# A conditional layer in quarters of the array, 512 columns at a time, turned by DMA

## The chip, the cores and the metric

The kernel runs on one core of one Trainium2 chip. The metric is the device time of one execution in microseconds: the median of 3 runs before the change is 2462.17 us (2460.88 to 2463.17). A separate, profiled execution gives the trace. Engines are named as in the profile: PE (TensorE) multiplies matrices, PEld is its weight load, DVE is VectorE, ACT is ScalarE, POOL is GpSimd, and SP issues most of the DMAs.

## What is computed

64 samples of 64 rows and 1024 columns pass one layer. Sample `b` is first multiplied by one of 16 small matrices, chosen by a list; then attention with 32 heads over 64 positions, an output projection with a residual, a second conditional layer and a quantised feed-forward follow. The change touches only the first step.

```python
W = weights[condition]                       # (64, 64, 64): one 64x64 matrix per sample
y = jnp.einsum('bct,bcd->bdt', x, W)         # the conditional layer
qkv = y @ attn_qkvw + attn_qkvb              # 1024 -> 3 x 1024
q, k, v = split_into_32_heads_of_32(qkv)
probs = softmax((q @ k.T) / sqrt(32))        # per sample and head, 64 x 64
x = x + (probs @ v) @ attn_ow + attn_ob
x = x + ffn(cond2(x))
```

All of this is in float32 up to the feed-forward.

## The kernel before

**Tiling.** The 4096 rows (tokens) go in 8 blocks of 512, and a block in four tiles of 128 rows, two samples each. A block's conditional output `y` is kept transposed, columns of `y` on the partitions, as four quarters `B11`, `B12`, `B21`, `B22` (first number: half of the 1024 columns; second: half of the block's 512 tokens). The projections to q, k and v use a Winograd-like scheme with seven products instead of eight; it needs four sums of the quarters, `T1` to `T4`. `T4` takes the place of `B12`.

**The conditional layer** (`conditional`, L339 on). For each tile j and half hf four matmuls (L355) hold 128 columns of x as weights and pass `wbd[j]`, a 128x128 matrix with the two samples' 64x64 matrices on its diagonal. The result arrives transposed, in one PSUM tile of 512 columns. DVE (L361) or ACT (L363) copies it into `yB`, and DVE makes the sums (L371, L376). POOL fills `wbd` in later blocks (L380), DVE in the first.

**Order of work.** Everything is issued from one program written out by hand. A planned clock `now` advances by a cost for each product on PE; `at(time, f)` puts work due at a planned time, and `run` issues what is due before the next product. An engine runs its own instructions strictly in this order. The order is thus fixed, and the times are only a plan: scores and contexts, for example, have no cost in it. Each block has four phases c = 0 to 3. A phase holds two groups of scores (L498), at its start and its middle, each for two of four units, and fills PE between them with projection jobs: q and k jobs of seven products of 1.72 us, v jobs of seven products of 3.43 us. Phase 0 has q, v and k; phases 1 and 2 have q and k; phase 3 has the next block's conditional layer, its first v job and its first q and k jobs.

A group goes: scores on PE; maximum, subtraction on DVE; exponent on ACT (L514); sum, reciprocal and product on DVE; `ph`, a split into 16-bit halves, on ACT (L528); `phT`, a DMA transpose issued by SP (L533); `pT`, the join of the halves, on ACT (L540), planned 8 us after the transpose; later the contexts on PE (L550) and `co` on ACT (L561). Contexts are taken two at a time, when two groups are ready, so some groups have none.

**Buffers that tie engines together.** Products go through four PSUM buffers (`ps_g`). In a q or k job ACT copies the first product (`psqp`, `pskp`, L406) and later takes the fifth, which lies in the same buffer, with its bias (`qT`, or four pieces of `kbd`, L419); the next job's first product needs that buffer again. The scores of a phase's first group read, in their second half, the `kbd` that ACT wrote. Contexts have two PSUM buffers (`ps_c`).

**Queues.** SP issues in program order the weights (`wq`, `wk`, 1.8 MB each, as soon as the job before the last is done; `wv`, 0.5 MB, after each v product), the x tiles (L246, four at a block's start) and the DMA transposes. POOL issues the gathers of the small matrices (L248) and runs side work ("chores") on the second layer's weights. The pool `xp` has four buffers.

Of the kernel before, what the change touches and what calls it, by code (L numbers as in the profile page):

```python
# [11 lines left out]
F32 = mybir.dt.float32  # L12
BF16 = mybir.dt.bfloat16
I32 = mybir.dt.int32
I16 = mybir.dt.int16
AF = mybir.ActivationFunctionType
ALU = mybir.AluOpType
# [3 lines left out]
P = 128  # L21
# [70 lines left out]
def planes(x):  # L92

    return x.bitcast(I16).rearrange("p (n h) -> p h n", h=2)
# [88 lines left out]
def attention(tc, a, x_t, ctx_d, ident, dram, ps_g, KC, PB, NBLK, NCH, HPC, H, C, chores, early, op):  # L183
# [6 lines left out]
    nc = tc.nc  # L190
    BLK = PB * P
    HB = BLK // 2
    KQ = KC // 2
    NP = NCH // 2
# [4 lines left out]
    cw = a["condw"].rearrange("s c d -> (s c) d")  # L199
# [11 lines left out]
    with ExitStack() as ctx, ExitStack() as mid:  # L211
        def pool(stack, name, bufs, **kw):
            return stack.enter_context(tc.tile_pool(name=name, bufs=bufs, reuse_waits="tile", **kw))
# [9 lines left out]
        yp = pool(mid, "y1", 1, side="right")  # L223
        p1 = pool(mid, "p1", 1, side="right")
        w = pool(early, "w1", 1)
        xp = pool(early, "xp", 4)


        cond_i = w.tile([P, KC * 4], I32, tag="cond_i", name="cond_i")
# [6 lines left out]
        nc.vector.tensor_copy(row_f, row_i)  # L236
        nc.vector.tensor_scalar(idx, cond_i, float(C), row_f, ALU.mult, ALU.add)

        def load_x(b):
            tiles = []  # L240
            for j in range(PB):
                i = b * PB + j
                xt = xp.tile([P, H], F32, tag="x", name=f"x_{i}")
                if i == PB - 1:
                    held(xt[:, 0:1], tiles[0][0])
                nc.sync.dma_start(xt, x_t[i])  # L246
                wg = xp.tile([P, C], F32, tag="wg", name=f"wg_{i}")
                nc.gpsimd.indirect_dma_start(  # L248
                    out=wg[:, :],
                    out_offset=None,  # L250
                    in_=cw,
                    in_offset=bass.IndirectOffsetOnAxis(ap=idx[:, i:i + 1], axis=0),
                )
                tiles.append((xt, wg))
            return tiles

        def held(word, other):


            nc.scalar.copy(word, other[:, 0:1])  # L260
# [24 lines left out]
        def load_qk(b, wh, c, eng=None):  # L285
            t = w_qk[b, wh, c] = wp.tile([P, 7, KQ, P], F32, tag="wqk", name=f"w{wh}_{b}_{c}")
            if b == 0:
                if (wh, c) == ("q", 0):
                    held(t[:, SLOT["A11"], 0, 0:1], x_next[0][1])
                for key in RAW:  # L290
                    nc.sync.dma_start(t[:, SLOT[key], :, :], quarter(key, (0 if wh == "q" else H) + c * P, P))
                return sums(
                    eng or nc.vector, lambda key: t[:, SLOT[key], :, :], lambda: nc.gpsimd.dma_start(qk_d[wh, c], t)
                )
            nc.sync.dma_start(t, qk_d[wh, c])
# [18 lines left out]
            return sums(eng, at, stored)  # L314

        bqkv = act.tile([P, 3 * KC], F32, tag="bqkv", name="bqkv")
        x_next = load_x(0)
        first_sums = load_qk(0, "q", 0) + load_qk(0, "k", 0, nc.gpsimd)
        nc.sync.dma_start(bqkv, a["qkvb_t"])
        first_sums += load_v_raw(0, nc.gpsimd)  # L320
# [1 line left out]

        wbd = []
        for j in range(PB):
            t = w.tile([P, P], F32, tag=f"wbd{j}", name=f"wbd{j}")
            nc.vector.memset(t, 0.0)
            wbd.append(t)
        kbd, vbd = [], []  # L330
        for u in range(4):
            t = act.tile([P, 2, HB], F32, tag=f"kbd{u}", name=f"kbd{u}")
# [6 lines left out]

        B = {}  # L340

        def conditional(b, tiles):

            def one(hf, j):
                key = f"B{hf + 1}{j // 2 + 1}"
                box = []

                def product():
                    xt = tiles[j][0]
                    if j % 2 == 0:  # L350
                        B[key] = yp.tile([P, KQ, HB], F32, tag=key, name=f"y{key}_{b}")
                    ps = ps_g.tile([P, 4, P], F32, tag="g", name=f"cond_{b}_{j}_{hf}")
                    for q in range(KQ):
                        k = hf * KQ + q
                        nc.tensor.matmul(ps[:, q, :], xt[:, k * P:(k + 1) * P], wbd[j], start=True, stop=True)  # L355
                    box.append(ps)

                def rest():
                    dst = B[key][:, :, (j % 2) * P:(j % 2 + 1) * P]
                    if j % 2 == 0:  # L360
                        nc.vector.tensor_copy(dst, box[0])  # L361
                    else:
                        nc.scalar.copy(dst, box[0])  # L363
                    if (hf, j) == (0, 3):
                        t_of("T1", "B12", "B11")
                    elif (hf, j) == (1, 3):
                        t_of("T2", "B22", "T1")
                        t_of("T3", "B22", "B12")
                    elif (hf, j) == (1, 1):
                        B["T4"] = B["B12"]  # L370
                        nc.vector.tensor_tensor(B["T4"], B["B21"], B["T2"], ALU.subtract)  # L371
                return 0.95, product, rest

            def t_of(key, x, y):
                B[key] = yp.tile([P, KQ, HB], F32, tag=key, name=f"{key}_{b}")
                nc.vector.tensor_tensor(B[key], B[x], B[y], ALU.subtract)  # L376

            for j, (_, wg) in enumerate(tiles):
                for r in range(2):
                    (nc.gpsimd if b else nc.vector).tensor_copy(wbd[j][halves[r], halves[r]], wg[halves[r], :])  # L380
            return [one(0, j) for j in range(PB)] + [one(1, j) for j in (2, 3, 0, 1)]

        def job(name, cost, n, matmuls, put, begin=None, done=None, order=ORDER):

# [186 lines left out]
        now = 0.0  # L571
# [3 lines left out]
        def at(time, f):  # L575
            heapq.heappush(due, (time, next(seq), f))
# [2 lines left out]

        def contexts(least=1):  # L580
            ready = sum(len(pTs) == 2 for *_, pTs in waiting)
            for n in range(ready if ready >= least else 0):
                context(*waiting.pop(0), 1.7 * n * (least - 1))

        def group(b, c, us):


            def begin():
                ps = scores(b, c, us)
                if behind:  # L590
                    behind.pop()()
                contexts(2)
                pTs = []
                waiting.append((b, c, us, pTs))
                for n, u in enumerate(us):
                    at(now + 1.7 * n, lambda n=n, u=u: first(u, ps[n], pTs))
                if b > 0:
                    at(now + 8.7, lambda: next(chores, None))
                    if c in (0, NP - 1):
                        at(now + 15, lambda: next(chores, None))  # L600

            def first(u, ps, pTs):
                p = exponents(b, c, u, ps)
                at(now + 3.4, lambda: normalize(b, c, u, p))
                at(now + 6.8, lambda: second(u, p, pTs))

            def second(u, p, pTs):
                h = parted(b, c, u, p)
                at(now + 1.7, lambda: third(u, turned(b, c, u, h), pTs))

            def third(u, hT, pTs):
                at(now + 8, lambda: pTs.append(joined(b, c, u, hT)))
            return begin
# [41 lines left out]
        def with_sums(fills, i, sums, count):  # L655
            cost, product, rest = fills[i]

            def product_and_sums():
                for _ in range(min(count, len(sums))):
                    sums.pop(0)()  # L660
                product()
            fills[i] = (cost, product_and_sums, rest)
# [14 lines left out]
                with_sums(js, 4, pending_sums, 4)  # L677
            return js

        for f in conditional(0, x_next):  # L680
            run(*f)
        for f in first_sums:
            f()
# [2 lines left out]
        for f in qk_fill(0, 0) + v_fill(0, 0):  # L686
            run(*f)
        for b in range(NBLK):
            if b + 1 < NBLK:
                x_next = load_x(b + 1)  # L690
            for c in range(NP):
                fills, length = [], None
                if c + 1 < NP:
                    fills += qk_fill(b, c + 1)
                    if c == 0:
                        fills[7:7] = v_fill(b, 1)
                        if b == 0:
                            for at_ in range(3, 7):
                                with_sums(fills, at_, v_raw, 1)
                elif b + 1 < NBLK:  # L700

                    fills += conditional(b + 1, x_next) + v_fill(b + 1, 0) + qk_fill(b + 1, 0)
                else:
                    behind.pop()()
                    mid.close()
                    op.open_rest()
                    fills += op.pair(0) + op.pair(1)
                    length = 24
                    at(now + 20, contexts)
                if b + 1 == NBLK and c == 1:  # L710
                    assert next(chores, None) is None
                    early.close()
                    for n, load in enumerate(op.open_weights()):
                        at(now + 5 * n, load)
                phase(b, c, fills, length or sum(f[0] for f in fills))
# [971 lines left out]
```

## Time and profile before

| | |
|---|---|
| median of 3 runs | 2462.17 us |
| profiled execution, whole / span | 2461.01 / 2459.1 us |
| mean granted clock of PE | 0.995 |
| attention blocks (68 to 1386 us): PE, DVE, ACT busy | 1315.9, 831.4, 547.3 of 1318 us |
| DMA share in the same stretch | 0.69 |
| PE, conditional layer L355 | 512 records, 61.7 us |
| ACT `ph` L528, `pT` L540 | 1047 ns, 1342 ns each |
| DVE `yB` L361, ACT `yB` L363 | 684 ns, 588 ns each |
| x tile, issue to landing | 9.1 us median, 512 KB |
| `wq`, `wk`, issue to landing | 7.7, 8.1 us median, 1792 KB |

A float32 matmul shows as two records on PE. "Idle before" names what an engine waited for just before an instruction. The times in the tables are those of the one profiled execution.

### The profile page before, as it was taken

The numbers are of one execution on the slowest core, as the hardware profiler recorded it, in microseconds if no ns is written. First come the engines' busy times: TensorE is split into PE (matmuls) and PEld (weight loads), VectorE is DVE, ScalarE is ACT, GpSimd is POOL, SyncE is SP. The second block draws the span as 40 slices with busy tenths as digits, with TensorE's granted clock in tenths as the row PEclk, the third lists the DMA queues.
The fourth block names the chain that finished last, engine by engine and source line by source line (L and its number), as shares of the span: only waits on it lengthen the run. The fifth ranks groups of instructions, "written<-read, shape, count | busy, mean of one in ns | idle before, by whom it ended". The sixth has DMA issues, their size and how long they took to land.

```text
span 2459.1 us, 34200 instructions
## 1 busy us (share of the span) xinstructions
PE 2423.2 (99%) x13194; PEld 1699.6 (69%) x13232; DVE 1533.1 (62%) x2957; ACT 952.8 (39%) x1303; POOL 363.4 (15%) x451
## 2 busy tenths in 40 slices
PE   8999999999999999999999999999999999999996
PEld 7888888888888888888888544444454545454452
DVE  4685585775664755745646623333367777778787
ACT  1353353342443533534424544344323333333333
POOL 5110001011122221210000233333200000000001
PEclk9999999999999999999999999999999999999998
DMA  8895767676677767775547588876744344434343
GB/s 280 284 264 152 219 200 238 188 208 210 201 198 250 206 194 246 207 208 175 177 137 234 170 258 255 263 243 215 242 126 83 84 79 88 80 81 87 70 95 72
DMA packets 417980, 446.76 MB, mean 182 GB/s; under 512 B 299665, under 2 KB 353938, under 8 KB 404114
## 3 DMA queue, kind: packets, MB, share of 16 engines
q1 hardware_dynamic: 387298, 377.90, 52.9%
q0 software_dynamic: 12080, 49.82, 7.7%
q10 hardware_dynamic: 18432, 16.79, 2.0%
q8 instruction: 106, 1.74, 0.3%
q14 instruction: 64, 0.52, 0.1%
HBM read 272.97 MB, written 100.66 MB: 152 GB/s over the span
## 4 chain that ended last, share of the span: by engine, by line
PE 94%; DVE 2%; ACT 2%; DMA 1%; issue 0%; ACTq 0%; SPq 0%; DVEq 0%
PE psva L462 5%; PE pska L435 5%; PE psvd L462 5%; PE psqa L435 5%; PE psvc L462 4%; PE pbc L1031 4%; PE pba L1031 4%; PE psqc L435 4%; PE pskc L435 4%; PE psqd L435 4%; PE pskd L435 4%; PE pbd L1031 4%; PE poa L1031 4%; PE pod L1031 4%; PE poc L1031 4%; PE s L498 3%
## 5 line engine op out<-in xcount | busy, mean ns | idle before, releaser
L540 ACT COPY pT<-phT 128x1024 int16<-128x1024 int16 x128 | 167.2, 1342 | 84.8 <-DMA phT<-ph 84.6
L514 ACT ACTIVATE prob<-prob 128x512 f32<-128x512 f32 x128 | 80.6, 630 | 259.4 <-DVE prob L511 232.1
L421 DVE SCALAR_TENSOR_TENSOR kbd<-pskd,bqkv,psku 32x256 f32<-32x256 f32 x256 | 123.1, 481 | 31.6 <-PE pskd L435 27.8
L528 ACT COPY ph<-prob 128x1024 int16<-128x1024 int16 x128 | 130.8, 1047 | 24.3 <-DVE prob L522 23.7
L1152 POOL TENSOR_TENSOR xo<-xo,ob 128x1024 f32<-128x1024 f32 x32 | 84.1, 2648 | 351.7 <-DVE To L1042 305.5
L561 ACT ACTIVATE co<-c,bqkv 128x256 f32<-128x256 f32 x128 | 60.1, 469 | 179.6 <-PE c L550 152.1
L435 PE MATMUL psqa<-yB,wq 128*128 128x256 f32 x512 | 123.6, 384 | 0.5 <-ACT psqp L406 0.5
L435 PE MATMUL pska<-yB,wk 128*128 128x256 f32 x512 | 122.6, 382 | 0.0
L1495 POOL DMA_DIRECT2D out_dram<-y x29 | 25.2, 869 | 652.3 <-DVE y L1487 652.3
L1126 ACT COPY xh<-xo 128x1024 int16<-128x1024 int16 x64 | 64.1, 1040 | 142.4 <-DVE xo L1171 142.4
L462 PE MATMUL psva<-wv,yB 128*128 128x256 f32 x512 | 117.0, 382 | 0.4
L1031 PE MATMUL poa<-woA,cx 128*128 128x512 f32 x256 | 115.4, 593 | 0.0
L1031 PE MATMUL pba<-wtA,x1T 128*128 128x512 f32 x256 | 115.1, 592 | 0.0
L1137 ACT COPY xTo<-xhT 128x1024 int16<-128x1024 int16 x64 | 84.7, 1339 | 58.4 <-DMA xhT<-xh 52.1
L435 PEld LDWEIGHTS pska<-yB,wk 128*128 128x128 f32 x512 | 96.0, 190 | 15.0 <-issue 2.6
L435 PEld LDWEIGHTS psqa<-yB,wq 128*128 128x128 f32 x512 | 95.2, 190 | 16.0 <-issue 2.8
L462 PEld LDWEIGHTS psva<-wv,yB 128*128 128x128 f32 x512 | 96.1, 190 | 14.1 <-ACT yB L363 1.0
L510 DVE TENSOR_REDUCE mx<-s 128x8 f32<-128x512 f32 x128 | 87.7, 685 | 10.7 <-PE s L498 9.3
L511 DVE TENSOR_TENSOR prob<-s,mx 128x512 f32<-128x512 f32 x128 | 88.5, 691 | 9.3 <-DVE mx L510 0.5
L522 DVE TENSOR_TENSOR prob<-prob,den 128x512 f32<-128x512 f32 x128 | 88.5, 692 | 4.4
L520 DVE TENSOR_REDUCE den<-prob 128x8 f32<-128x512 f32 x128 | 86.7, 678 | 7.2 <-ACT prob L514 6.3
L1031 PEld LDWEIGHTS poa<-woA,cx 128*128 128x128 f32 x256 | 48.4, 190 | 60.1 <-issue 59.9
(243 smaller groups left out, 5135.5 us busy)
## 6 DMA issues: line engine op xcount, KB each, us to landing
wv<-v_d SPq DMA_DIRECT2D x98, 512.0 KB, 3.9
wq<-q_d SPq DMA_DIRECT2D x28, 1792.0 KB, 7.7
wk<-k_d SPq DMA_DIRECT2D x28, 1792.0 KB, 8.1
x<-in_x_dram SPq DMA_DIRECT2D x32, 512.0 KB, 9.1
ctx_d<-co ACTq DMA_DIRECT2D x128, 128.0 KB, 4.2
cx<-ctx_d SPq DMA_DIRECT2D x16, 1024.0 KB, 6.9
xo<-in_x_dram SPq DMA_DIRECT2D x32, 512.0 KB, 5.7
xT_d<-xTo SPq DMA_DIRECT2D x64, 256.0 KB, 3.2
```

Source lines behind the costliest of these rows:

```text
L421: nc.vector.scalar_tensor_tensor(dst, ps, bias, u, ALU.add, ALU.add)
L435: nc.tensor.matmul(ps[:, 0:HB], A[:, SLOT[A_OF[i]], k, :], B[B_OF[i]][:, k, :], start=first and k == 0, stop=k == KQ - 1, skip_group_check ...
L462: nc.tensor.matmul(ps[:, j * VC:(j + 1) * VC], B[B_OF[i]][:, k, j * P:(j + 1) * P], A[:, k, :], start=first and j == 0 and k == 0, stop=k ...
L510: nc.vector.tensor_reduce(mx_v, ps, AX.X, ALU.max)
L511: nc.vector.tensor_tensor(p.rearrange("p (a e) k -> p a e k", a=2), ps, mx_v.unsqueeze(3).to_broadcast([P, 2, HPC, C]), ALU.subtract)
L520: nc.vector.tensor_reduce(den, p, AX.X, ALU.add)
L522: nc.vector.tensor_tensor(p, p, den.unsqueeze(2).to_broadcast([P, n, C]), ALU.mult)
L528: nc.scalar.copy(h, planes(p.rearrange("p n k -> p (n k)")))
L540: nc.scalar.copy(planes(pT.rearrange("p a b q -> p (a b q)")), hT)
L1031: self.nc.tensor.matmul(ps, self.B[self.B_OF[i]][:, k, :], self.A[self.A_OF[i]][:, k, :], start=first and k == 0, stop=k == self.KQ - 1, s ...
L1137: nc.scalar.copy(planes(xT.rearrange("p k q -> p (k q)")), hT)
L1152: nc.gpsimd.tensor_add(s["x"][:, t, :], s["x"][:, t, :], self.ob)
```

## The change

The first block's conditional layer stays as it is. For later blocks it becomes one call per tile, `conditional_tile`, and the tiles are spread over the block before. The small matrices are now the weights: four matmuls with 64x64 weights, one in each quarter of the array, pass 512 columns of x each. Their result is not transposed; so ACT splits it into 16-bit halves (`yh`, one buffer), SP issues a DMA transpose (`yhT`), and ACT joins the halves into the quarter of `y`. For the second half of the columns the two samples lie crosswise, and the join takes two copies. The plan puts the transpose 1.7 us after the split, and the join 5.1 us after the transpose.

A tile is issued in a group that takes no contexts, right after its scores, and once in each block's phase 0 as a fill of its own. It uses the two `ps_c` buffers, and after its matmuls it loads the x tile two ahead. Quarters now have two sets of buffers, one for even and one for odd blocks; `xp` has two x buffers. The sums T1 to T4 move to the end of phase 2 and the first two products of phase 3. Phase 3 has no conditional layer any more. At the start x tiles 2 and 3 and `wbd` borrow buffers of quarters, and the four memsets of `wbd` become one of 128x1024.

```diff
-        xp = pool(early, "xp", 4)
+        xp = pool(early, "xp", 2)
...
-        wbd = []
-        for j in range(PB):
-            t = w.tile([P, P], F32, tag=f"wbd{j}", name=f"wbd{j}")
-            nc.vector.memset(t, 0.0)
-            wbd.append(t)
+        wbd = yp.tile([P, KC, P], F32, tag="B21", name="wbd")
+        nc.vector.memset(wbd, 0.0)
...
+        def conditional_tile(b, j):
+            xt, wg = x_of.pop((b, j))
+            ps = [ps_c.tile([P, 2, HB], F32, tag="c", name=f"cond{hf}_{b}_{j}") for hf in range(2)]
+            for hf in range(2):
+                for r in range(2):
+                    nc.tensor.matmul(
+                        ps[hf][halves[r ^ hf], :, :], wg[halves[r], :], xt[halves[r], hf * 512:(hf + 1) * 512],
+                        start=True, stop=True,
+                    )
+            if j + 2 < PB:
+                load_x(b, j + 2)
+            elif b + 1 < NBLK:
+                load_x(b + 1, j + 2 - PB)
+
+            def parted_y(hf):
+                h = w.tile([P, 2, 512], I16, tag="yh", name=f"yh_{b}_{j}_{hf}")
+                nc.scalar.copy(h, planes(ps[hf].rearrange("p a t -> p (a t)")))
+                at(now + 1.7, lambda: turned_y(hf, h))
+
+            def turned_y(hf, h):
+                hT = w.tile([P, 2, 512], I16, tag="yhT", name=f"yhT_{b}_{j}_{hf}", bufs=2)
+                nc.sync.dma_start(
+                    hT.rearrange("p h (k q) -> p (h k) q", q=P), h.rearrange("p h t -> p (h t)"), transpose=True
+                )
+                at(now + 5.1, lambda: joined_y(hf, hT))
+
+            def joined_y(hf, hT):
+                key = f"B{hf + 1}{j // 2 + 1}"
+                if j % 2 == 0:
+                    Y[key] = quarter_of(b, key)
+                src = hT.rearrange("p h (k q) -> p h k q", q=P)
+                for r in range(2) if hf else (slice(0, P),):
+                    q = halves[r ^ hf] if hf else r
+                    q = slice((j % 2) * P + q.start, (j % 2) * P + q.stop)
+                    dst = Y[key].bitcast(I16).rearrange("p k (q h) -> p h k q", h=2)[:, :, :, q]
+                    nc.scalar.copy(dst, src[:, :, :, halves[r] if hf else r])
+
+            at(now + 1.7, lambda: parted_y(0))
+            at(now + 5.1, lambda: parted_y(1))
...
-                contexts(2)
+                if not contexts(2) and (b, c, us[0]) != (0, 0, 0):
+                    next_tile()
...
+            if b == 0:
+                load_x(1, 0)
+                load_x(1, 1)
             if b + 1 < NBLK:
-                x_next = load_x(b + 1)
+                tiles_to_come += [(b + 1, j) for j in range(PB)]
...
+                        n = 7 if b else 14
+                        fills[n:n] = [(0.9, next_tile, None)]
+                    if c + 2 == NP and b + 1 < NBLK:
+                        sums_to_come = [lambda b=b, n=n, Y=Y: t_of(b + 1, Y, *T_OF[n]) for n in range(4)]
+                        with_sums(fills, -2, sums_to_come, 1)
+                        with_sums(fills, -1, sums_to_come, 1)
                 elif b + 1 < NBLK:
-                    fills += conditional(b + 1, x_next) + v_fill(b + 1, 0) + qk_fill(b + 1, 0)
+                    assert len(Y) == 6 and not tiles_to_come
+                    fills += v_fill(b + 1, 0) + qk_fill(b + 1, 0)
+                    with_sums(fills, 0, sums_to_come, 1)
+                    with_sums(fills, 1, sums_to_come, 1)
+                    B = Y
+                    Y = {}
```

## The prediction

> **What bounds the kernel now.** I read four views, from coarse to fine: the page, PE in order of time round one conditional layer, the groups of the `phT` and `cond` tiles, and ACT in order of time in one k job. First the page: busy shares, the slices, the chain that ended last.
>
> ```profile
> PE 2423.2 (99%) x13194; PEld 1699.6 (69%) x13232; DVE 1533.1 (62%) x2957; ACT 952.8 (39%) x1303; POOL 363.4 (15%) x451
> ...
> PE   8999999999999999999999999999999999999996
> ...
> PEclk9999999999999999999999999999999999999998
> ...
> PE 94%; DVE 2%; ACT 2%; DMA 1%; issue 0%; ACTq 0%; SPq 0%; DVEq 0%
> ```
>
> PE is busy 99%, its clock is granted in full almost throughout, and 94% of the chain is PE. So PE time taken out of the attention blocks shortens the span, and a wait that reaches PE lengthens it one for one. A block takes 170 us (conditional layers start at 691.27, 861.37 and 1031.47 us).
>
> PE in order of time at the last such layer (start, duration, line, tiles):
>
> ```profile
> 1198.98 1.10 PE L498 MATMUL s<-kbd,qT 64*64 64x128 f32 x32
> 1200.01 2.08 PE L550 MATMUL c<-pT,vbd 128*64 128x64 f32 x64
> 1202.03 7.53 PE L355 MATMUL cond<-wbd,x 128*128 128x128 f32 x64
> 1209.68 3.72 PE L462 MATMUL psva<-wv,yB 128*128 128x256 f32 x16
> ```
>
> Each matmul has two records. The layer lasts 1209.68 - 1202.03 = 7.65 us for 32 matmuls of 128 columns; read in the same way the seven later layers last 8.33, 7.25, 7.65, 7.25, 7.25, 7.60 and 7.65, together 53.0 us. The scores above it are the model for the new form: 16 matmuls 64*64, four quarters of the array, in 1.03 us, where 16 of 128 columns one after the other would take 16 x 0.237 = 3.8 us. Four quarters do run at once.
>
> The other resource is the DMA turn. All 128 of before:
>
> ```profile
> L533 SPq DMA_TRANSPOSE phT<-ph x128: 1231/1263/3589, 75.0 to 1417.6; - x128
> L540 ACT COPY pT<-phT x128: 1323/1342/1371, 85.1 to 1424.8; 128x1024 int16<-128x1024 int16 x128
> ...
>   DMA phT<-ph: 84.6, 22
> ...
> DMA to landing us min/median/max: 3.0/3.5/7.5
> ```
>
> A turn lands in 3.0 to 7.5 us. ACT waited for 22 of 128, though the join is emitted 8 us (of the plan) after the turn. In those 22 the time from issue to the start of the copy is 3.5 to 7.2, median 4.5; the issue at 621.36 with its copy at 625.67 is one of 4.31.
>
> Last, ACT in a k job of block 3, the stretch where the change will be tight:
>
> ```profile
> 648.95 0.63 ACT L514 ACTIVATE prob<-prob 128x512 f32<-128x512 f32 x1 [5.57 <-DVE prob L511]
> 650.34 0.63 ACT L514 ACTIVATE prob<-prob 128x512 f32<-128x512 f32 x1 [0.76 <-DVE prob L511]
> 650.88 0.35 ACT L406 COPY pskp<-pska 128x256 f32<-128x256 f32 x1
> 651.13 2.54 ACT L540 COPY pT<-phT 128x1024 int16<-128x1024 int16 x2
> 653.53 1.99 ACT L528 COPY ph<-prob 128x1024 int16<-128x1024 int16 x2
> 656.23 1.91 ACT L419 ACTIVATE kbd<-pska,bqkv 32x256 f32<-32x256 f32 x4 [0.71 <-PE pska L435]
> ```
>
> PE's scores before this stood at 646.25, the next ones at 659.57. These read in their second half the `kbd` that ACT ends at 658.14: ACT is 39% busy over the span, yet its slack here is 1.4 us and half a scores group.
>
> **The change part by part** (later blocks 1 to 7, 28 tiles of 128 rows).
>
> *PE, removed:* 53.0 us. *Added:* 28 tiles of four 64*64 matmuls with 512 columns. A 256-column f32 matmul takes 0.432 us (psva: 8 in 3.45), so 512 take 0.86, and four at once 0.86. The scores hold four rounds of 0.216 = 0.86 and last 1.03, so going in and out of quarters costs 0.17. Three tiles of a block follow scores directly and share that: 0.90 each; one stands alone: 1.03. A block: 3.73; seven: 26.1. PE gains 26.9 us. If quarters ran only two at a time a tile would last 1.75 and this gain be about 4; that bound stays in the range.
>
> TensorEngine Tiling (Array Packing) of the Trainium skill, "Gotcha 1: PSUM Pressure", speaks against this: different row tiles must not use one PSUM bank at the same time. In the scores the upper rows write one bank and the lower rows another; in the new tile both row halves write `ps[0]`, then both `ps[1]`, so no row of before shows it. By that rule the four would need three turns, 2.6 us a tile, and the sum would be a loss of about 20 us instead of the gain; I go by the scores' row, as the two writes lie on different partitions.
>
> *ACT, added a tile:* two `yh` parts like `ph` (1.05 each), one whole join like `pT` (1.34), two half joins (about 0.77 each by its rate): 5.0 us, 20 a block, against four `yB` copies of 0.59 taken away. ACT has room for that on average (70.7 of 170). What counts is order. `yh` has one buffer, so the second part waits until the first has been turned, and everything behind it on ACT waits too. With 4.5 us a turn, counted from the scores' start:
>
> - Tile in the second group of c=1 (k job): exponents to 3.3, `yh` 0 to 4.4, second exponents 5.0, `pskp` 5.4, `pT` 6.7, wait for the turn until 8.9, `yh` 1 to 9.95, `pT` 11.2, two `ph` 13.3, join 14.55, `kbd` x4 (1.9) 16.4. PE arrives at the next scores at 1.03 + 0.95 + 7 x 1.73 = 14.1 and needs that `kbd` at 14.6. PE stands 1.9 us. A turn of 3.5 makes it 0.9, one of 7.5 makes it 4.9.
> - Tile of the first group of c=0 (q job): the wait ends at 10.1, `ph` x2, join, `qT` end at 15.1; the next v product needs that PSUM bank at 15.1: 0.2 us, and 3 at a turn of 7.5.
> - First group of c=1: the same 15.1 against 16.1: nothing; 2 at 7.5.
> - Lone tile of c=0: 3.45 us v products leave room; its turns stand on SP behind `wv` loads that wait for PE, and the second `pT` ends near 29.4, against 31 where the context needs it. Nothing.
>
> Block 0 has its tiles elsewhere, one of them also in a k job; I count it like the others. Together 2.1 a block, 7 x 2.1 = 14.7 us. The ends: 0, if nothing reaches PE, and 9.9 x 7 = 69, if every turn takes 7.5.
>
> *SP queue:* 56 more turns of 1.23 us issue; x loads go from four at the block's start to one after each tile, waiting for that tile's matmuls. What stands behind them are the tile's own turns and later `ph` turns; weights are loaded one job ahead (issue to landing 7.7 to 8.1 us, needed 14 later), so I put nothing beyond the waits above. The 1.8 MB weight load issued as the job starts still runs when the turn is issued; therefore 4.5 and not the median 3.5. *POOL:* 28 gathers of about 1 us move with the x loads, 56 `wbd` copies go; a gather is asked for two tiles ahead and POOL is 15% busy: nothing; if a chore in front blocked it for 20 us (the longest `cs` wait is 19.5) the tile would still come later. *DVE:* 28 copies of 0.68 go. The four sums of a block (1.22 each) move into the end of the last k job and the first v products. That k job holds about 12.6 us of DVE work in 13.1, so DVE runs some 2 us late; the first sum read is T2, 7 us later, in v's second product: nothing, and up to 2 us a block if that cover is gone. *Start:* one `wbd` memset twice as long as the four (0.59 us); the copies behind it wait for the gather anyway until 9.04: 0, at most 0.6.
>
> **Sum.** -26.9 + 14.7 + at most 0.6 (taken as 0.3) = -11.9 on the profiled execution's 2461.0 (span 2459.1 and 1.9 round it): 2449.1. The median of the runs shown stands 1.2 above that execution: 2450.
>
> **The rivals.**
>
> *The cover holds.* For it: 106 of 128 turns were never waited for, and a quiet turn takes 3.0 to 3.5. Then 0.5 us a block is lost: -26.9 + 3.5 = -23, 2439. Against it: weight loads stand just in front of the turns.
>
> *The turn becomes the bound (slower).* One place: the second `yh` behind the single buffer. Stalls grow by one to three us a block for each us of a turn; they eat 26.9 when they reach 3.8 a block, at a turn of about 5.5. At 6.5: 3.9 + 2.2 + 1 = 7.1, x 7 = 50, so +23: 2485. For it: 7.2 was seen. Against it: the median of the late ones is 4.5.
>
> *Quarters do not run together.* Three turns a tile: 28 x 2.6 = 73 + 3 against 53 is +23, while PE's delay gives ACT back most of its lateness: 2485. Two at a time: near 2466. For it: no row has both row halves in one bank. Against it: the scores' 1.03.
>
> **How the numbers follow.** Forecast 0.45 (2450, own range 2441 to 2460), cover holds 0.20 (2439), turn as bound 0.20 (2485), quarters apart 0.15 (0.12 at 2485, 0.03 at 2466). Within 0.2% (4.9 us, about what a measurement of this kernel can tell) is 2457 to 2467. Faster: 0.39 of the forecast and 0.20; slower: 0.17 of the turn and 0.12; the rest, 0.12, is the same. Range 2437 to 2485; the ends of the unknown terms, 2435 with no wait at all and 2504 with every turn at 7.5 us, lie a little and far outside, and I leave them out.
>
> **What would show it.** Tile matmuls 64*64 64x512 of 0.9 to 1.05 us from first to next line, blocks of about 168.5 us; ACT idle before `yh` for DMA `yhT`, some 2 to 4 us on every tile; PE waits at the scores for ACT `kbd`, about 2 us once a block; the `cond` group of 7.25 to 8.33 only in block 0. I am wrong if tiles take 1.7 us or more, if PE waits for `kbd` are absent or above 4 us, if `phT` turns land much later than before, or if DVE's sums hold up v's second product.

## The result

| | before | after |
|---|---|---|
| median | 2461.71 us (6 runs, 2460.82 to 2463.17) | 2526.74 us (6 runs, 2521.05 to 2535.18) |
| profiled execution / span | 2461.01 / 2459.1 us | 2521.05 / 2519.3 us |
| first to last scores (the attention) | 1318.8 us | 1376.6 us |
| mean granted clock of PE | 0.995 | 0.984 |

The ratio is 1.0268, 95% interval 1.0255 to 1.0281: slower by 65 us. The forecast was 2450, with a range up to 2485. Line numbers below are those of the changed kernel: scores L552, contexts L604, tile matmuls L396, `yh` L407, `yhT` L412, its joins L426, `ph` L582, `phT` L587, `pT` L594, `kbd` L473, weight load L294, x load L244.

The page after, in the lines that stood in the prediction:

```profile
PE 2428.1 (96%) x12970; PEld 1672.0 (66%) x13008; DVE 1513.0 (60%) x2926; ACT 1054.2 (42%) x1415; POOL 347.6 (14%) x395
...
PE   8999999989889899899999999999999999999996
...
PEclk9999999999999999999999999999999999999998
...
PE 86%; DMA 6%; ACT 4%; DVE 2%; issue 1%; SPq 0%; ACTq 0%; DVEq 0%
```

PE is below 90% busy in six slices now, between the ninth and the twentieth, all in the attention, and the chain that ended last runs 10% through DMA and ACT instead of 3%. The waits of PE and of ACT name the place (us in total, times, longest):

```profile
PE s L552 <- ACT kbd L473: 38.3, 15, 7.4
PE c L604 <- ACT yh L407: 10.6, 3, 6.3
...
ACT yh L407 <- DMA yhT<-yh: 182.9, 28, 15.9
```

28 waits of ACT: each tile's second `yh` waits for the tile's first turn (the DMA transpose `yhT`), 6.5 us on average. Here is one such wait from end to end, in block 3, second group of phase 1. PE in order of time (start, duration, line, tiles):

```profile
679.32 1.10 PE L552 MATMUL s<-kbd,qT 64*64 64x128 f32 x32
680.24 1.04 PE L396 MATMUL cond<-x,wg 64*64 64x512 f32 x8
681.21 1.99 PE L489 MATMUL pska<-yB,wk 128*128 128x256 f32 x8
...
693.50 0.67 PE L552 MATMUL s<-kbd,qT 64*64 64x128 f32 x16
701.40 0.69 PE L552 MATMUL s<-kbd,qT 64*64 64x128 f32 x2 [7.23 <-ACT kbd L473]
702.37 1.12 PE L552 MATMUL s<-kbd,qT 64*64 64x128 f32 x14 [0.28 <-ACT kbd L473]
703.42 3.68 PE L604 MATMUL c<-pT,vbd 128*64 128x64 f32 x64
```

The tile (680.24) takes 0.97 us up to the next job, so its four quarters do run together. But the next scores, begun at 693.50, stand for 7.23 us in front of their second half, for `kbd`. ACT in the same stretch:

```profile
684.22 1.36 ACT L594 COPY pT<-phT 128x1024 int16<-128x1024 int16 x1
695.23 1.01 ACT L407 COPY yh<-cond 128x1024 int16<-128x1024 int16 x1 [9.65 <-DMA yhT<-yh]
696.14 1.33 ACT L594 COPY pT<-phT 128x1024 int16<-128x1024 int16 x1
697.33 1.98 ACT L582 COPY ph<-prob 128x1024 int16<-128x1024 int16 x2
699.22 1.32 ACT L426 COPY yB<-yhT 128x1024 int16<-128x1024 int16 x1
700.41 1.90 ACT L473 ACTIVATE kbd<-pska,bqkv 32x256 f32<-32x256 f32 x4
```

ACT stands for 9.65 us at the second `yh`, with `pT`, two `ph`, a join and `kbd` queued behind it. And SP, which issues the DMAs:

```profile
679.09 1.24 SPq L587 DMA_TRANSPOSE phT<-ph  x1
680.43 1.49 SPq L166 DMA_DIRECT2D cq<-in_ow_dram  x2
682.03 1.27 SPq L587 DMA_TRANSPOSE phT<-ph  x1
683.39 0.55 SPq L294 DMA_DIRECT2D wq<-q_d  x1
684.04 0.39 SPq L244 DMA_DIRECT2D x<-in_x_dram  x1
684.52 12.98 SPq L412 DMA_TRANSPOSE yhT<-yh  x2
```

The tile before had already held up ACT at its own second `yh` (4.11 us), so `ph` and with it the `phT` turns came late; SP works in order, so the 1.8 MB weight load, whose buffer PE had left at 679.3, went out at 683.39, the 0.5 MB x load at 684.04, and the turn at 684.52, 1.1 us behind the weight load. Its last packet landed 10.2 us after its issue.

### The profile page after: what moved, and what is told of

Same layout as the page of the kernel before. It is cut to its first block, busy times and chain, and to the rows that moved or that the text cites. A ratio compares the mean times of both kernels' runs of the same rounds, so it can differ in the third digit from the quotient of the medians.

```text
span 2519.3 us, 33934 instructions
## 1 busy us (share of the span) xinstructions
PE 2428.1 (96%) x12970; PEld 1672.0 (66%) x13008; DVE 1513.0 (60%) x2926; ACT 1054.2 (42%) x1415; POOL 347.6 (14%) x395
## 4 chain that ended last, share of the span: by engine, by line
PE 86%; DMA 6%; ACT 4%; DVE 2%; issue 1%; SPq 0%; ACTq 0%; DVEq 0%
PE psva L516 5%; DMA yhT<-yh 4%; PE psqa L489 4%; PE pbc L1102 4%; PE pba L1102 4%; PE pbd L1102 4%; PE psqc L489 4%; PE psqd L489 4%; PE poa L1102 4%; PE pod L1102 4%; PE poc L1102 4%; PE psvc L516 4%; PE psvd L516 4%; PE pska L489 3%; PE pskc L489 3%; PE pskd L489 3%
## 5 line engine op out<-in xcount | busy, mean ns | idle before, releaser
L594 ACT COPY pT<-phT 128x1024 int16<-128x1024 int16 x128 | 167.2, 1341 | 67.1 <-DMA phT<-ph 66.7
L475 DVE SCALAR_TENSOR_TENSOR kbd<-pskd,bqkv,psku 32x256 f32<-32x256 f32 x256 | 123.1, 481 | 35.2 <-PE pskd L489 31.4
L407 ACT COPY yh<-cond 128x1024 int16<-128x1024 int16 x56 | 56.5, 1009 | 183.5 <-DMA yhT<-yh 182.9
L582 ACT COPY ph<-prob 128x1024 int16<-128x1024 int16 x128 | 128.3, 1043 | 7.2 <-DVE prob L576 6.2
L552 PE MATMUL s<-kbd,qT 64*64 64x128 f32 x2048 | 80.8, 283 | 38.4 <-ACT kbd L473 38.3
L552 PEld LDWEIGHTS s<-kbd,qT 64*64 64x64 f32 x2048 | 59.3, 136 | 65.2 <-ACT kbd L473 43.5
```

The lines of the kernel that those rows point to most:

```text
L475: nc.vector.scalar_tensor_tensor(dst, ps, bias, u, ALU.add, ALU.add)
L552: nc.tensor.matmul(ps[halves[r], hp, n, jj * 2:(jj + 1) * 2, :], q_of[b, c][halves[hp], m, t * HB + t0:t * HB + t0 + C], kbd[u][halves[hp] ...
L582: nc.scalar.copy(h, planes(p.rearrange("p n k -> p (n k)")))
L594: nc.scalar.copy(planes(pT.rearrange("p a b q -> p (a b q)")), hT)
```

## The experiments

Theory 1: the turn, right behind a load, lasts 10 us; the single `yh` buffer makes ACT stand still for it; `kbd` and the scores are late by that. Rival theory 2: the added ACT work of splits and joins is at fault (56.5, 38.8 and 37.5 us, 133 in all; the expectations estimate it at 137) and not the wait. In each comparison the kernel before ran on the same chip (2460.5 to 2464.2 us).

**Without the turn.** In `turned_y` the DMA is left out, and the joins read `still`, a tile set to zero once, so blocks 1 to 7 go on with zeros:

```diff
-                hT = w.tile([P, 2, 512], I16, tag="yhT", name=f"yhT_{b}_{j}_{hf}", bufs=2)
-                nc.sync.dma_start(
-                    hT.rearrange("p h (k q) -> p (h k) q", q=P), h.rearrange("p h t -> p (h t)"), transpose=True
-                )
+                hT = still
```

> The DMA turn of yh is left out, and with it the wait for it: the joins read a tile of zeros, so that the conditional layer's result of blocks 1 to 7 is left out (zeros take its place). TensorE's quarters, the 56 splits and the 84 join copies on ACT stay as they are. Theory 1: without the turns no ACT wait is left: 2440 us (2434 to 2455). Theory 2 (ACT work alone): 2500 to 2530. Between, 2455 to 2500: ACT work carries part of it.

Measured: 2443.09 us, 0.9916 of before (0.9899 to 0.9932). From first to last scores it takes 1297.0 us against 1376.6 in the changed kernel. The ACT work alone costs next to nothing (3.6 us beside the next run); theory 2 falls.

**TensorE alone.** Split, turn and join are left out:

```diff
-            at(now + 1.7, lambda: parted_y(0))
-            at(now + 5.1, lambda: parted_y(1))
+            if j % 2 == 0:
+                for hf in range(2):
+                    key = f"B{hf + 1}{j // 2 + 1}"
+                    Y[key] = quarter_of(b, key)
+                    nc.gpsimd.memset(Y[key], 0.0)
```

> The quarters of TensorE stay, and split, turn and join are left out (POOL sets the result of the conditional layer of blocks 1 to 7 to zero instead): what TensorE alone gains. Prediction's sum for TensorE: 27 less, by the measured 0.98 us a tile 25.4 less: 2437 us (2433 to 2442). If the copies and chains on ACT had hidden cost that the quarters also relieve, lower.

Measured: 2439.12 us, 0.9910 (0.9895 to 0.9925). From first to last scores 1293.4 us instead of 1318.8: 25.4 less, where 53.0 - 28 x 0.98 is 25.6. So in the profiled executions the changed kernel loses 83 us (1376.6 - 1293.4) of what its quarters would give, and 80 of them (1376.6 - 1297.0) go with the turn. PE is idle for 57 of the 83 us, against 0.8 us with TensorE alone; most of the rest is a lower clock behind the waits (last section).

**Two buffers, later joins: three runs.** Two `yh` buffers needed room, which came from `co`:

```diff
-        cop = pool(ctx, "co1", 4, side="right")
+        cop = pool(ctx, "co1", 2, side="right")
...
-                h = w.tile([P, 2, 512], I16, tag="yh", name=f"yh_{b}_{j}_{hf}")
+                h = w.tile([P, 2, 512], I16, tag="yh", name=f"yh_{b}_{j}_{hf}", bufs=2)
```

> The split halves yh get two buffers instead of one (room is made by two instead of four buffers of co); the joins stay 5.1 us behind the issue of their turn. Theory 1 (the turn goes out right behind a load of 1.8 MB that SP issues late, its data take 10 us, and ACT stands still at the second yh, with kbd and the scores behind it): the wait of 182.9 us at yh goes to nearly 0, but ACT then stands at the first join, 5.1 us behind an issue that takes 10; about half of the loss remains: 2480 us (2460 to 2505). Theory 2 (it is the 137 us of ACT work of splitting and joining, not the wait, that delays kbd and the contexts): no more than 10 us gained, 2515 to 2530. Theory 3 (the single buffer alone is the cause, and a turn that has nobody waiting in front of it is short): 2436 to 2450.

The second run has only the later join, the third both:

```diff
-                at(now + 5.1, lambda: joined_y(hf, hT))
+                at(now + 8, lambda: joined_y(hf, hT))
```

> yh keeps its one buffer; the joins are planned 8 us behind the issue of their turn instead of 5.1. Theory 1: the second yh still waits for the first turn, so little changes: 2515 to 2530 us, the wait at yh stays above 150 us. Theory 2 (ACT work): the same work, merely later, 2510 to 2535. Rival to both (ACT stands at the joins): the time falls below 2490.

> Both: two buffers of yh (and two of co), joins 8 us behind the issue of the turn. Theory 1: ACT waits neither at yh nor at the joins for more than 2 us each, the scores of the phase after the next have their kbd in time, and nearly the whole gain of 25 us on TensorE is left: 2440 us (2434 to 2460), faster than the kernel before. Theory 2: 2505 to 2530. If the late loads on SP also hurt somebody else (the weights themselves come late), the waits of PE for q and k weights show it, 2460 to 2480.

Measured: two buffers 2486.98 (1.0096, 1.0079 to 1.0112), later joins 2521.22 (1.0233, 1.0216 to 1.0250), both 2486.38 (1.0090, 1.0068 to 1.0112). Later joins alone change little, as theory 1 said. The first run lies in theory 1's range, but not for its reason: ACT waited 35.5 us at the joins, and the third run, in which that is down to 1.4, takes the same time. And both together should have given 2440. The waits of ACT and PE in the third run:

```profile
ACT co L615 <- DMA ctx_d<-co: 83.6, 33, 8.6
...
PE psqa L489 <- ACT psqp L460: 20.8, 9, 3.9
```

The wait at `yh` was down to 7.0 us, but ACT now waited 83.6 us for the writes of `co`, with `psqp`, and then PE, behind it. I had counted the two buffers of `co` as free.

**Two buffers in the x tile.** The halves are written over the x tile that PE has read, which needs no room; the x load that reuses the tile moves behind them:

```diff
-            if j + 2 < PB:
-                load_x(b, j + 2)
-            elif b + 1 < NBLK:
-                load_x(b + 1, j + 2 - PB)
+            def load():
+                if j + 2 < PB:
+                    load_x(b, j + 2)
+                elif b + 1 < NBLK:
+                    load_x(b + 1, j + 2 - PB)
...
-                h = w.tile([P, 2, 512], I16, tag="yh", name=f"yh_{b}_{j}_{hf}")
+                h = xt.bitcast(I16)[:, hf * H:(hf + 1) * H].rearrange("p (h t) -> p h t", h=2)
...
-                at(now + 5.1, lambda: joined_y(hf, hT))
+                at(now + 8, lambda: joined_y(hf, hT))
...
             at(now + 5.1, lambda: parted_y(1))
+            at(now + 15, load)
```

> With two buffers of yh the wait at yh was gone, but the room came from the buffers of co, and ACT then waited 83.6 us for the writes of co, with PE behind it at psqd and psqa (the excess over the usual group durations was still 39.5 us). Here yh gets its two buffers without touching co: the halves are written over the x tile that the four quarters have read, and the x load that reuses this tile is planned 15 us behind the tile; joins 8 us behind the issue of the turn. Theory 1 (late turn and single buffer; the remainder in the previous runs is the cut of co): 2440 us (2435 to 2455), faster than the kernel before, no wait of PE above 2 us at scores or contexts but for the first one. Rival (the remainder belongs to the joins' ACT work or to the turns' load on the DMA, not to co): 2475 to 2490 as with two buffers of co.

Measured: 2439.08 us (5 runs, 2436.32 to 2439.86), 0.9913 of before (0.9899 to 0.9926): faster than both kernels, and the time of TensorE alone. The same stretch of block 3, SP, then ACT, then PE (`yh` is called `x` here; its line is L408, `kbd` L475, the turn L413):

```profile
638.21 0.34 SPq L294 DMA_DIRECT2D wq<-q_d  x1
638.66 0.36 SPq L244 DMA_DIRECT2D x<-in_x_dram  x1
642.36 5.70 SPq L413 DMA_TRANSPOSE yhT<-x  x2
```

```profile
644.27 1.35 ACT L596 COPY pT<-phT 128x1024 int16<-128x1024 int16 x1
645.47 1.03 ACT L408 COPY x<-cond 128x1024 int16<-128x1024 int16 x1
646.37 1.36 ACT L596 COPY pT<-phT 128x1024 int16<-128x1024 int16 x1
647.57 2.01 ACT L584 COPY ph<-prob 128x1024 int16<-128x1024 int16 x2
649.45 1.91 ACT L475 ACTIVATE kbd<-pska,bqkv 32x256 f32<-32x256 f32 x4
```

```profile
652.29 1.10 PE L554 MATMUL s<-kbd,qT 64*64 64x128 f32 x32
653.32 2.09 PE L606 MATMUL c<-pT,vbd 128*64 128x64 f32 x64
```

Nobody waits for the turn; since `ph` is punctual, the weight load leaves at 638.21, right after PE let go of its buffer, 4.15 us ahead of the turn, whose last packet lands 6.1 us after its issue.

**Which part of it.** Three runs each put one thing back: one `yh` buffer of its own, two buffers of `co`, joins at 5.1 (the edits are against that version).

```diff
-                h = xt.bitcast(I16)[:, hf * H:(hf + 1) * H].rearrange("p (h t) -> p h t", h=2)
+                h = w.tile([P, 2, 512], I16, tag="yh", name=f"yh_{b}_{j}_{hf}")
```

> As the version with yh in the x tile (x load 15 us behind its tile, joins 8 us behind the issue of the turn, four buffers of co), with one difference: yh is again one buffer of its own. If the single buffer is what turns the late turn into lost time, nearly all of the loss is back: 2515 us (2500 to 2525). If the later x load and the later joins did the work in that version: 2440 to 2460.

```diff
-        cop = pool(ctx, "co1", 4, side="right")
+        cop = pool(ctx, "co1", 2, side="right")
```

> As the version with yh in the x tile, which took 2439 us, with one difference: two buffers of co instead of four. If the cut of co is what cost the two runs with a second yh buffer their 47 us: 2485 us (2475 to 2495), and ACT waits some 80 us for the writes of co. If it was the x load at its old place: 2439 to 2450.

```diff
-                at(now + 8, lambda: joined_y(hf, hT))
+                at(now + 5.1, lambda: joined_y(hf, hT))
```

> As the version with yh in the x tile, with one difference: joins 5.1 us behind the issue of the turn, as in the changed kernel, instead of 8. In the trace of that version the turns landed in 5.2 us (median) and 7.7 (longest), so that joins at 5.1 us would stand for up to 2.6 us each, some 28 tiles by 1 to 2 us of ACT, which TensorE mostly does not feel: 2443 us (2438 to 2458). If a wait of ACT is passed on to TensorE wherever it stands: 2465 to 2490.

Measured: 2505.36 (1.0160, 1.0143 to 1.0177), 2490.09 (1.0107, 1.0084 to 1.0130) and 2446.21 (0.9929, 0.9911 to 0.9946). The difference of the ratios to 0.9913, times 2462 us, makes it 61 us for the single buffer alone, 48 for the cut of `co` alone and 4 for the early joins, whose interval overlaps that of the version with late ones. In the second of them ACT waits 96.8 us for the writes of `co`, so that explanation holds too. In the first the two waits of the changed kernel are back, at `yh` and at the scores:

```profile
ACT yh L408 <- DMA yhT<-yh: 158.0, 29, 16.6
```

```profile
PE s L554 <- ACT kbd L475: 26.1, 15, 5.8
```

**What makes the turn long.** Three runs on the changed kernel itself. The x load alone 15 us later (`load` holds the two `load_x` calls as above):

```diff
             at(now + 5.1, lambda: parted_y(1))
+            at(now + 15, load)
```

> The changed kernel (one yh, joins at 5.1 us) with one edit: the 0.5 MB x load is planned 15 us behind its tile instead of right at it, so that only the 1.8 MB weight load stands directly in front of the turns. If the weight load is what makes a turn last 10 us: 2505 to 2525. If the x load in front of the turn does it: 2460 to 2490. In proportion to the bytes (0.5 of 2.3 MB) a fifth of the 65 us: about 2512.

The weight load in two parts:

```diff
-            nc.sync.dma_start(t, qk_d[wh, c])
+            nc.sync.dma_start(t[:, 0:4, :, :], qk_d[wh, c][:, 0:4, :, :])
+            at(now + 10.5, lambda: nc.sync.dma_start(t[:, 4:7, :, :], qk_d[wh, c][:, 4:7, :, :]))
```

> The changed kernel (one yh, joins at 5.1 us, x load at once) with one edit: of each 1.8 MB weight load four of the seven parts go out at the old place and three 10.5 us later, so that 1.0 instead of 1.8 MB stands in front of the first turn of a tile. If the bytes in front set the length of the turn (10 us behind 2.3 MB): 2500 us (2485 to 2515), the turns behind a load 6 to 8 us. If the turn is long for another reason: 2520 to 2530, and 2540 or more if the later parts come late for TensorE.

The weight load on another queue:

```diff
-            nc.sync.dma_start(t, qk_d[wh, c])
+            nc.gpsimd.dma_start(t, qk_d[wh, c])
```

> The changed kernel with one edit: the 1.8 MB q and k weight loads of blocks 1 to 7 go out on POOL's queue instead of SP's. If order on SP's queue is the cause (SP held by late ph turns, the load then just in front of the turn): the load leaves when PE frees its tile, the turns wait for the x loads alone, 2455 to 2490. If it is the sharing of the 16 DMA engines by the load and the turn: turns still last 7 to 10 us and the time stays at 2500 to 2530.

Measured: 2516.48 (1.0216, 1.0200 to 1.0232), 2512.98 (1.0207, 1.0179 to 1.0236) and 2557.92 (1.0384, 1.0368 to 1.0400). I read from the packets how long the first turn took from issue to last packet for the tile that matters most (second group of phase 1, mean of blocks 1 to 5, counted from 0): 9.5 us in the changed kernel, 8.9 without the 0.5 MB in front, 8.0 without 0.77 MB of the weights. That does not show that the bytes in front count, though: the weight load also stood further ahead of the turn in these two runs, 2.9 and 2.5 us on average instead of 1.7. From the issue of the load to the turn's last packet it is 11.2, 11.8 and 10.5 us, so the 0.5 MB show nothing and the 0.77 MB at most 0.7 us. In the version with `yh` in the x tile both loads stood in front in full, the weights 4.15 us ahead, and the turn took 6.1: a load further ahead goes with a shorter turn. The time of the two runs follows only in part, as the single buffer still waits for a turn of 8 to 9 us.

The third run I had wrong. The `yhT` turn of this tile did get shorter (6.4 us on average, with the load 8.3 us ahead of it; in block 1, with the load 3.9 us ahead, it took 10.5), but the load did not stop hurting; it hurt the turn next to it. In block 2 the load goes out on POOL at 531.57. SP and ACT:

```profile
533.23 9.54 SPq L587 DMA_TRANSPOSE phT<-ph  x1
542.83 1.43 SPq L244 DMA_DIRECT2D x<-in_x_dram  x1
```

```profile
545.37 1.34 ACT L594 COPY pT<-phT 128x1024 int16<-128x1024 int16 x1 [8.59 <-DMA phT<-ph]
550.37 1.01 ACT L407 COPY yh<-cond 128x1024 int16<-128x1024 int16 x1 [3.65 <-DMA yhT<-yh]
```

A `phT` turn 1.7 us behind the load occupies SP for 9.54 us, and `pT` waits 8.59; the wait has changed its name.

The longest wait of that run stands elsewhere, near the end of block 0. Two weight loads on POOL landed 23.9 and 29.0 us after their issue (7.0 to 9.8 in the changed kernel), four `phT` turns held SP for 46.62 us, and the scores stood 28.54 us for `kbd`:

```profile
PE s L552 <- ACT kbd L473: 73.1, 20, 28.5
```

In the changed kernel this row has 38.3 us, so that one wait is most of what PE waits there beyond the changed kernel (the profiled run, with 2572.6 us, is the slowest of its four). Why these two loads took so long is not shown.

Order on SP's queue alone is thus not what makes a turn long; what fits this run and the changed kernel, though nothing here proves it, is that the turn and the load share the DMA engines, on whichever queue the load goes. The Trainium skill, DMA: Bandwidth & Descriptors, "Queues, rings and completion order", has a rule that would make it so: each DMA engine takes turns between its queues packet by packet. The trace agrees in so far as a turn of many small packets gained nothing from a queue without the load (the 9.54 us above); it does not show the queues alternating.

Not tried: a turn placed ahead of the weight load.

## Why the prediction was wrong

- **Quarters on PE: right.** Forecast 0.90 and 1.03 us a tile, measured 0.97 and 1.02; the gain 25.4 instead of 26.9 us. The rule of TensorEngine Tiling (Array Packing), "Gotcha 1: PSUM Pressure", that I had weighed against the scores' row cost no time here: both row halves wrote one bank and the four matmuls still ran together. The rival of quarters apart falls.
- **The term that failed is the stall of 14.7 us (2.1 a block).** PE stood idle for 57 us in the attention instead, and with the half clock behind the waits, for which the sum had no term, the loss is 83. Three steps of the term were wrong:
  - *"With 4.5 us a turn".* The prediction counts from the issue to the start of the copy that waits. Counted so, the first groups of phases 0 and 1 took 5.1 on average in blocks 1 to 5 (4.5 to the last packet), but the second group of phase 1, the one that reaches PE, took 10.1 (9.5 to the last packet). The chain behind the turn was right: 4.9 us of stall at a turn of 7.5, and one more for each us, make 7.5 at 10.1, and the scores waited 6.1 to 7.4 us there in blocks 2 to 5. I had the 1.8 MB load 4 us ahead of the turn, by the plan; in block 3 it went out 1.1 us ahead. A load that takes about 8 us to land (7.7 and 8.1 in the rows of before), still in flight, was the row to price this turn by, not the median of the late `phT` turns of before, none of which had a 1.8 MB load in the 8 us in front of it.
  - *"SP queue ... nothing beyond the waits above".* SP runs in order, so a late `ph` holds back the weight load behind it. The first tile's wait at `yh` thereby pushes the load into the next tile's turn: the stall feeds itself. That is why the end of 2504 (every turn at 7.5 us), which I had left out of the range, was not even an end. Where ACT does not wait, in the version with `yh` in the x tile, the load left 4.15 us ahead in each of blocks 1 to 5.
  - *"Lone tile of c=0 ... Nothing".* In blocks 1 to 5 SP issued its first turn 7.0 us after `yh` was ready and the turn took 7.1 us more to its last packet. Contexts, which need the same PSUM buffers, waited 10.6 us for `yh` in all.
- **The rival "the turn becomes the bound" was the mechanism**: one place, the second `yh` behind the single buffer. Its price, 2485 at a turn of 6.5, was too low, as the turns that counted took 10.1. So was its chance of 0.20: "weight loads stand just in front of the turns" was what I had written against the cover, and it speaks for this rival as much.
- **Costed at nothing, and rightly:** POOL, the sums on DVE and the start. TensorE alone and the version with yh in the x tile have all of these, and both take 2439.
- **What would show it:** ACT idle before `yh` came as said, but 6.5 us a tile instead of 2 to 4; the waits of the scores for `kbd` came as said, up to 7.4 us instead of about 2.

## What to carry to other kernels

A DMA that others wait for is priced by what is in flight when it is issued in the order that the queues really have, and not by its own kind's median; moving the big load to another queue here only moved the wait to the turn next to it. An engine that works in order and waits at a single buffer passes a delay to everything queued behind it, so before work is added there, give the buffer a second half, if possible in memory that is just dead, as the x tile was here: with that the change gains 0.9% instead of losing 2.7%. Room taken from another ring of buffers is not free because that ring was never waited for: the row that shows no wait shows it with the buffers it has.

## What the hardware did that I had not expected

After a long wait PE did not go on at full speed. The changed kernel by stretches around the wait in block 3 (columns: stretch, its length, busy time and instructions of PE, PEld, DVE, ACT and POOL, then the granted clock, DMA share and GB/s):

```profile
680.00:693.00 13.00, 13.00 (x79) 10.79 (x72) 9.54 (x19) 5.02 (x8) 2.66 (x5) 1.00 0.97 269
693.00:703.00 10.00, 2.48 (x32) 1.51 (x33) 2.75 (x6) 7.70 (x11) 0.00 (x0) 0.74 0.57 109
703.00:707.00 4.00, 4.00 (x74) 3.58 (x67) 2.67 (x4) 1.67 (x4) 2.47 (x5) 0.50 1.01 315
707.00:720.00 13.00, 13.00 (x66) 11.12 (x68) 4.89 (x11) 7.11 (x10) 0.48 (x2) 0.96 0.62 180
```

The granted clock is 1.00 before the wait and 0.50 right behind it; the contexts at 703.42 took 3.61 us to the next job, where 2.01 is usual. The wait thus cost at least 1.6 us more than its own length. The Trainium skill, TensorE: Matmul & The Clock Gate, part on the HAM clock gate, gives half clock after an idle window of about 3.4 us; the 7.23 us here agree with that. In the same trace the clock is 0.50 also from 1005.0 to 1008.4, behind waits of 2.49 and 0.55 us, so shorter waits can cost clock here too; a wait of 1.82 us, which ended at 821.17, was followed by no such drop. From the first to the last scores the clock stands at 0.50 for 58 us in all, and PE works in 42 of them. That makes an estimate of 21 us lost at half speed, beside the 57 us of waiting; about 5 of the 83 us stay unexplained. My price of a PE wait, "one for one", was too low for long ones.

And a turn costs its issuing queue more than the 1.23 us of a quiet one: issued beside the 1.8 MB load it kept SP for 9.54 us, and everything behind it on SP waited that long, even with the load on another queue.
